# Reordered opening, accumulators in pairs of PSUM banks, and one wide VectorE rescale in a macaron feed-forward / S4 kernel

## The chip, the cores and the metric

The kernel runs on one core of one Trainium2 chip. The metric is the device time of one execution in microseconds (us), from the first to the last instruction and the little that lies around them. A change of 0.2% or less can't be told from none here.

## The reference

The input u has shape (2, 1024, 1024). Read as 2048 rows of 1024, it goes through three residual parts: half of a gated feed-forward of the layer-normed input, an S4 sequence convolution of the layer-normed input, and the same feed-forward again.

```python
def _dequant(qweight, scales, qzeros, g_idx):
    shifts = jnp.arange(PACK, dtype=jnp.uint32) * BITS        # PACK 8, BITS 4
    w = (qw[:, None, :] >> shifts[None, :, None] & MAXQ).reshape(-1, qweight.shape[1])
    z = ((qz[:, :, None] >> shifts[None, None, :] & MAXQ) + 1).reshape(qzeros.shape[0], -1)
    return (w.astype(scales.dtype) - z[g_idx].astype(scales.dtype)) * scales[g_idx]
...
h = jax.nn.silu(xf @ Wg) * (xf @ Wu)                          # 1024 -> 2752
out = h @ Wd                                                  # 2752 -> 1024
...
y = jnp.fft.irfft(jnp.fft.rfft(u, n=n) * jnp.fft.rfft(K, n=n), n=n)[..., :L]
return y + D[0] * u                                           # K from the S4 parameters
...
x = x + 0.5 * _L0_ffn_ref(_layernorm(x, axis=-1), ...)
x = x + _L0_attn_ref(_layernorm(x, axis=-1), ...)
x = x + 0.5 * _L0_ffn_ref(_layernorm(x, axis=-1), ...)
```

The feed-forward weights are 4-bit, with a scale and a zero point for each group of 128 input rows (8 groups for gate and up; 21 for down, whose last 64 rows share the last group). Everything is in float32.

## The kernel before

**Jobs.** The 2048 rows are four blocks of 512 (`TB`). Each block passes the feed-forward twice, so there are eight jobs (`JOBS`, line 1069). Jobs 0, 1, 4, 5 are the first feed-forward of blocks 0 to 3, jobs 2, 3, 6, 7 the second. `fast()` walks through the jobs; each is a `gate_up` stage and a `down` stage. What lies between two feed-forwards of a block (moments, normalizing, transposes, convolution, saving) is hung as hooks on the steps of the neighbouring jobs' stages: `at(up, s, f)` runs f at step s of gate/up, `at(dn, d, f)` at step d of down. The convolution of jobs 1, 2, 5 and 6 is such a hook, and the S4 tables are built in job 1.

**Weights.** In job 0 the packed words are fetched (`fetch`, line 365), split into nibbles (`split`), and made into integers minus zero points (`dequantize`, line 391), without the scale. The result goes to DRAM (`w_q`), and each job reads it back tile by tile (`load_w`, three steps ahead, six buffers in `wpool`). The zero points are first turned from packed words to a table in DRAM (`zero_points`, line 209) and read back spread over the rows (`fetch_zeros`). Down weights follow the same way in hooks of job 0.

**Precision and scales.** Each activation is split in two pieces, `xTh` (fp32r) and `xTl` (the rest), so that each product is two matmuls of 128x128 by 128x512. The scale of a group is applied by Horner's rule on the accumulator in PSUM: after group g the accumulator is multiplied by the ratio `rat` of scale g to scale g+1 (`scaled`, line 475), and the matmuls of the next group add on top. So every step has matmul, rescale, matmul, rescale on one accumulator; ScalarE rescales at line 477, VectorE at line 479.

**Gate/up.** 43 columns of 128 (21 gate, 21 up, one of two halves of 64) are done in eight waves: five of three gate/up couples, three of two, the last with the half unit besides. A wave has eight steps, one for each group; a step has four to six units, gate and up in turn (`order`, line 493). A unit is an accumulator of one PSUM bank, 128x512 float32; the pool `acc` has six, the pool `ps` the other two banks, which transposes and small products use. Even units are rescaled by ScalarE, odd ones by VectorE; in job 0 also the odd unit at position 1 goes to ScalarE, except at g = 3. After the last group `gated` (line 521) makes silu of the gate accumulator on ScalarE, the product with the up accumulator on VectorE, and the two pieces on GpSimd.

**Down.** Two halves of 512 output columns, each 22 row blocks with four accumulators `po` (line 559), rescaled in the same way by `ratd`.

**The order of work.** [...] The order on each engine is set by a scheduler when the program is built, from priorities, dependencies and its own estimates, and it also places the waits on semaphores. It keeps track of which tile each instruction reads and writes. SP issues nearly all DMAs; in the opening ScalarE's queue issues some of them too.

**The opening** (lines 1160 to 1187) loads the zero-point words on ScalarE's queue (three DMAs into one tile, which GpSimd clears first), the block's four row tiles and the first packed words on SP's; then come moments, subtraction of the mean on ScalarE (`less_mean`), eight dequantizations of the first weight tile, whose first row is also stored straight into `first_tile` by ScalarE's queue (line 399), the scaling by the deviation, and the transposes (`turn`).

Of the kernel before, what the change touches and what calls it, by code (L numbers as in the profile page):

```python
# [9 lines left out]
F32 = mybir.dt.float32  # L10
# [5 lines left out]
ALU = mybir.AluOpType  # L16
AX = mybir.AxisListType
PSUM = bass.MemoryType.PSUM
DRAM = bass.MemoryType.DRAM
# [30 lines left out]
def macaron_s4_kernel(  # L50
# [43 lines left out]
    ypool = ctx.enter_context(tc.tile_pool(name="y", bufs=4))  # L94
    apool = ctx.enter_context(tc.tile_pool(name="acc", bufs=6, space=PSUM))
    ppool = ctx.enter_context(tc.tile_pool(name="ps", bufs=2, space=PSUM))
# [4 lines left out]

    def acc(name):
        return apool.tile([P, 512], F32, tag="acc", name=name)

# [8 lines left out]
    row_t = const.tile([P, 1], F32, tag="row", name="row_t")  # L113
    shift_t = const.tile([P, 1], I32, tag="shift", name="shift_t")


# [51 lines left out]

    def turned(n, half, name, bank=bank):

        ps = bank(name)
        for k in range(4):
            nc.tensor.transpose(ps[:, bass.ts(k, P)], n[:, bass.ts(4 * half + k, P)], ident)  # L173
        return ps.rearrange("p (c t) -> p c t", c=4)
# [4 lines left out]
    def turn(b, t, n, half, bank=bank):  # L179
        k = ln[b, t][2]  # L180
        if b not in pieces:
            pieces[b] = [
                xtpool.tile([P, NC, TB], F32R, tag="xT", name=f"xT{w}_{b}_{k}") for w in ("h", "l")
            ]
        hi, lo = (a[:, 4 * half : 4 * half + 4, bass.ts(t, P)] for a in pieces[b])
        ps = turned(n, half, f"pt_{b}_{k}_{t}_{half}", bank)
        nc.scalar.copy(hi, ps)  # L187
        nc.vector.tensor_tensor(lo, ps, hi.bitcast(F32), ALU.subtract)  # L188
# [19 lines left out]

    def zero_points():

        n, nd = INTER // 8 // SEG, HID // 8 // SEGD
        z = t2("zq").bitcast(I32)[:, : n + nd]
        nc.gpsimd.memset(z, 0)
        for i, src in enumerate((gate_qz, up_qz)):
            own = slice(GK * SEG * i, GK * SEG * (i + 1))
            nc.scalar.dma_start(z[own, :n], src.rearrange("g (s n) -> (g s) n", s=SEG))
        nc.scalar.dma_start(z[: GD * SEGD, n:], down_qz.rearrange("g (s n) -> (g s) n", s=SEGD))
        zi = t4("zi").bitcast(I32)[:, : 8 * (n + nd)]
        for k in range(8):
            nc.vector.tensor_scalar(  # L220
                zi.rearrange("p (a k) -> p k a", k=8)[:, k, :],
                z,
                4 * k,
                15,
                ALU.logical_shift_right,
                ALU.bitwise_and,
            )
        tab = t2("ztab").bitcast(BF16)[:, : 8 * (n + nd)]
        nc.vector.tensor_scalar(tab, zi, 1.0, None, ALU.add)
        nc.scalar.dma_start(z_dram.rearrange("g (s n) -> (g s) n", s=SEG), tab[:, : 8 * n])  # L230
        nc.scalar.dma_start(
            zd_dram.rearrange("g (s n) -> (g s) n", s=SEGD), tab[: GD * SEGD, 8 * n :]
        )

# [156 lines left out]
    def dequantize(w, j):  # L391

        parts, z = packed[w]
        q = wpool.tile([P, width_of(w)], F32R, tag="w", name=f"q_{w}_{j}")
        src = parts[j % 2][:, j // 2, :]
        nc.vector.tensor_tensor(q, src, z, ALU.subtract)  # L396
        dst = w_q[w].rearrange("(r j) n -> j r n", j=8)[j]
        if w == 0:
            nc.scalar.dma_start(first_tile[j:P:8].bitcast(F32), q[: P // 8].bitcast(F32))
        nc.sync.dma_start(dst, q.bitcast(F32))  # L400
        if j == 7:
            packed.pop(w)
# [31 lines left out]
    def first_weights(up, dn, at):  # L434


        for w in range(1, len(WAVES)):
            s0 = 8 * w - 12
            at(up, max(0, s0 - 3), lambda w=w: (fetch(w), fetch_zeros(w)))
            at(up, max(0, s0 - 1), lambda w=w: split(w))  # L440
            for j in range(8):
                s = s0 + j if w > 1 else (1, 2, 2, 3, 3, 3, 4, 4)[j]
                at(up, s, lambda w=w, j=j: dequantize(w, j))
        s0 = len(STEPS) - 12
        when = lambda n: (up, s0 + n) if n < 12 else (dn, (5 * (n - 12)) // 6)
        for n in range(6 * 8):
            k, j = divmod(n, 8)
            a, rt = divmod(k, 3)
            if j == 0:
                at(*when(max(0, n - 3)), lambda a=a, rt=rt: fetch_down(a, rt))  # L450
                at(*when(max(0, n - 1)), lambda a=a, rt=rt: split_down(a, rt))
            at(*when(n), lambda a=a, rt=rt, j=j: dequantize_down(a, rt, j))

    AHEAD = 3

    def load_w(j, s):
# [24 lines left out]
    def gate_up(j, b, hooks):  # L481
        hi, lo = pieces[b]
        ps = {}
        ready = {s: load_w(j, s) for s in range(AHEAD)}
        for s, (wi, g) in enumerate(STEPS):
            if s + AHEAD < len(STEPS):
                ready[s + AHEAD] = load_w(j, s + AHEAD)
            for hook in hooks.get(s, ()):
# [7 lines left out]
            for pos, (unit, col) in enumerate(order):  # L496
                if g == 0:
                    ps[unit] = acc(f"pg_{j}_{unit}")
                p = ps[unit]
                for k, part in enumerate((lo, hi)):  # L500
# [7 lines left out]
                    )  # L508
                if g < GK - 1:
                    on_act = unit % 2 == 0 or (j == 0 and pos == 1 and g % 4 < 3)  # L510
                    if unit == 2 * WIDE:
                        on_act = g % 2 == 0
                    scaled(on_act, p, p, rat[:, unit, g : g + 1])
                elif unit == 2 * WIDE:
# [33 lines left out]
    def down(j, b, hooks):  # L548
# [3 lines left out]
        for d, (a, f) in enumerate(steps):  # L552
# [5 lines left out]
            if f == 0:  # L558
                ps = [acc(f"po_{j}_{a}_{c}") for c in range(4)]
            for c in range(4):  # L560
# [284 lines left out]
    def turn_whole(n, name):  # L845
        s = t4(name).rearrange("p (c t) -> p c t", c=NC)
        for half in range(2):
            ps = turned(n, half, f"{name}_{half}")
            dst = s[:, 4 * half : 4 * half + 4, :]
            if half:  # L850
                nc.vector.tensor_copy(dst, ps)
            else:
                nc.scalar.copy(dst, ps)
# [5 lines left out]
    def general():  # L859
# [146 lines left out]
        def feed_forward(b, k):  # L1006
# [6 lines left out]
            for f in range(NF):  # L1013
                m = width(f)
                got = []
                for i in range(2):
                    ps = acc(f"pf_{b}_{k}_{f}_{i}")
                    for a in range(2):
# [3 lines left out]
                        for j in range(4):  # L1022
# [3 lines left out]
                            )  # L1026
                    got.append(ps)
                g = gpool.tile([P, TB], F32, tag="g", name=f"gf_{b}_{k}_{f}")
# [4 lines left out]
            for t0 in range(0, NT, 2):  # L1033
                ps = {(t, nh): acc(f"pd_{b}_{k}_{t}_{nh}") for t in (t0, t0 + 1) for nh in range(2)}
                for f in range(NF):
# [35 lines left out]
    def fast():  # L1071
        for j, (b, k) in enumerate(JOBS):
# [47 lines left out]
            if j == 0:  # L1120
                for s, k0, k1 in ((2, 3, 11), (12, 11, 19), (20, 19, WIDE)):
                    at(up, s, lambda k0=k0, k1=k1: scales(k0, k1, scale_rows(k0, k1)))
                at(up, 28, scales_down)
                for t in range(NT):
                    at(up, t, lambda t=t: turn(0, t, first[t], 1))
                first_weights(up, dn, at)
            if j == 1:
                tables = s4_tables()
                for s in range(2, 42):
                    at(up, s, lambda: next(tables, None))  # L1130
            if j == 2:
                at(up, 30, in_order)
            if after:
# [12 lines left out]
                for t in range(NT):  # L1146
                    at(dn, o + 1 + 4 * t, lambda t=t: anorm(t))
                    at(dn, o + 2 + 4 * t, lambda t=t: turn(ab, t, an[t], 0))
                    at(dn, o + 4 + 4 * t, lambda t=t: turn(ab, t, an[t], 1))
            at(dn, 21, lambda: load_x(b, rows_of(u, b) if k == 1 else saved(b)))  # L1150
# [8 lines left out]

    zero_points()  # L1160
    x[0] = [t4(f"x_0_{t}") for t in range(NT)]
    for t, src in enumerate(rows_of(u, 0)):
        nc.sync.dma_start(x[0][t], src)
        if t == 1:
            fetch(0)
    fetch_zeros(0)
    srow = scale_rows(0, 3, nc.scalar)
    first = []

    def less_mean(t, m):  # L1170

        n = t4(f"xn_0_1_{t}")
        nc.scalar.activation(n, x[0][t], AF.Identity, bias=m, scale=-1.0)
        first.append(n)
        if t == 1:
            split(0)

    moments(0, 1, less_mean)
    deviations(0, 1, -1.0)
    for i in range(8):  # L1180
        dequantize(0, i)
    scales(0, 3, srow)
    for t in range(NT + 1):
        if t < NT:
            nc.scalar.activation(first[t], first[t], AF.Copy, scale=ln[0, t][1])  # L1185
        if t:
            turn(0, t - 1, first[t - 1], 0, acc)
    x.pop(0)
# [87 lines left out]
```

## Time and profile before

| what | us |
|---|---|
| median of 3 runs | 2219.82 |
| lowest and highest | 2217.35, 2220.73 |
| the profiled execution, its own time | 2220.67 |
| its span, first to last instruction | 2218.9 |
| first product of gate/up starts at | 35.44 |
| gate/up of jobs 0 to 7 | 190.3, 214.5, 196.4, 159.9, 159.8, 194.6, 194.7, 159.8 |
| down of jobs 0 to 7 (the last with the end of the program) | 102.6, 86.0, 86.4, 86.5, 85.9, 86.0, 85.9, 94.2 |

The stage lengths are the distances between the first products of line 501 (gate/up) and line 562 (down) on TensorE's timeline. The profile is of one execution. Its page gives the busy time of each engine; a group's row has the line, the engine, the operation, output and input by name and shape, the count, the busy time and the mean in ns of one, then the idle time ahead of it and what ended most of that. A wait "A <- B" says that A stood idle until B was done. Matmuls are pipelined, so their durations overlap, and the distance of their starts says more than their sum.

### The profile page before, as it was taken

What the parts mean: (1) busy time and instruction counts of PE and PEld (TensorE: products, weight loads), DVE (VectorE), ACT (ScalarE), POOL (GpSimd) and SP (SyncE); (2) the same over time, 40 slices, a digit from 0 to 9 for tenths busy, and PEclk for the clock granted to TensorE, in tenths of its full rate; (3) what the DMA queues carried; (4) which work ended last, traced back from release to release, by engine and by line L of the source; (5) the groups of instructions that cost most, each with busy time, mean ns of one, the idle gap of its engine ahead of it and who ended that gap; (6) DMA issues with size and microseconds to landing.
All of it is one profiled execution on the core that took longest, in us unless ns stands there. A gap on an engine that the chain in (4) does not pass through costs nothing.

```text
span 2218.9 us, 28013 instructions
## 1 busy us (share of the span) xinstructions
PE 2134.2 (96%) x9364; PEld 1683.4 (76%) x9364; DVE 1712.8 (77%) x2792; ACT 1452.8 (65%) x2229; POOL 328.8 (15%) x350
## 2 busy tenths in 40 slices
PE   4898889999999999999999999999999999999998
PEld 3676667867887778888788878877788777888876
DVE  7898869767786878877887777867788677777776
ACT  5776776545764677677767777646676467767775
POOL 0232002211011230122102320102201023012210
PEclk9999999999999999999999999999999999999999
DMA  7788784434443545644455444434444354554444
GB/s 238 271 261 274 233 250 131 141 96 150 135 149 107 174 135 173 225 146 136 142 185 187 126 138 138 150 104 159 138 136 146 108 180 134 156 189 144 135 136 130
DMA packets 163667, 359.91 MB, mean 162 GB/s; under 512 B 22395, under 2 KB 27588, under 8 KB 163518
## 3 DMA queue, kind: packets, MB, share of 16 engines
q1 hardware_dynamic: 162730, 357.47, 51.8%
q8 instruction: 78, 1.28, 0.2%
q10 hardware_dynamic: 788, 0.58, 0.1%
q14 instruction: 71, 0.58, 0.1%
HBM read 306.86 MB, written 50.73 MB: 161 GB/s over the span
## 4 chain that ended last, share of the span: by engine, by line
PE 51%; issue 35%; DMA 5%; DVE 5%; POOL 3%; ACT 1%; SPq 0%; ACTq 0%; DVEq 0%; POOLq 0%
PE pg L501 35%; PE po L562 9%; PE pc L835 5%; POOL hl L530 2%; POOL hh L528 1%; DMA w<-wq 1%; DMA wd<-wdq 1%; DMA wdq<-qd 1%; DVE pg L479 1%; DVE hf L526 1%; DVE q L396 1%; PE st L173 1%; DMA wq<-q 1%; PE pt L173 0%; PE pb L583 0%
## 5 line engine op out<-in xcount | busy, mean ns | idle before, releaser
L477 ACT ACTIVATE pg<-pg,rat 128x512 f32<-128x512 f32 x1256 | 820.1, 662 | 467.0 <-PE pg L501 462.4
L501 PE MATMUL pg<-xTl,w 128*128 128x512 f32 x2752 | 1084.3, 396 | 27.9 <-DVE pg L479 12.2
L501 PE MATMUL pg<-xTh,w 128*128 128x512 f32 x2752 | 1070.9, 391 | 0.0
L479 DVE TENSOR_TENSOR pg<-pg,rat 128x512 f32<-128x512 f32 x1152 | 785.8, 696 | 162.9 <-PE pg L501 154.1
L501 PEld LDWEIGHTS pg<-xTl,w 128*128 128x128 f32 x2752 | 517.8, 188 | 164.1 <-DVE pg L479 22.6
L501 PEld LDWEIGHTS pg<-xTh,w 128*128 128x128 f32 x2752 | 518.6, 188 | 103.3 <-issue 0.2
L562 PE MATMUL po<-hl,wd 128*128 128x512 f32 x1344 | 538.2, 403 | 18.4 <-DVE po L479 7.7
L477 ACT ACTIVATE po<-po,ratd 128x512 f32<-128x512 f32 x670 | 438.7, 662 | 170.1 <-PE po L562 169.8
L562 PE MATMUL po<-hh,wd 128*128 128x512 f32 x1344 | 521.3, 392 | 0.0
L479 DVE TENSOR_TENSOR po<-po,ratd 128x512 f32<-128x512 f32 x610 | 419.1, 697 | 93.5 <-PE po L562 89.2
L528 POOL CAST hh<-hf 128x512 fp32r<-128x512 f32 x168 | 109.4, 651 | 1755.1 <-DVE hf L526 1630.5
L562 PEld LDWEIGHTS po<-hl,wd 128*128 128x128 f32 x1344 | 252.1, 188 | 96.4 <-DVE po L479 18.4
L562 PEld LDWEIGHTS po<-hh,wd 128*128 128x128 f32 x1344 | 253.4, 189 | 46.0
L530 POOL TENSOR_TENSOR hl<-hf,hh 128x512 fp32r<-128x512 f32 x168 | 222.9, 1327 | 13.5
L526 DVE SCALAR_TENSOR_TENSOR hf<-pg,rat,g 128x512 f32<-128x512 f32 x168 | 125.1, 748 | 78.6 <-PE pg L501 32.6
L523 ACT ACTIVATE g<-pg,rat 128x512 f32<-128x512 f32 x168 | 115.6, 689 | 41.8 <-PE pg L501 39.2
L835 PE MATMUL pc<-toeplitz,st 128*128 128x512 f32 (+3 forms) x384 | 126.5, 486 | 0.0
L835 PEld LDWEIGHTS pc<-toeplitz,st 128*128 128x128 f32 x384 | 70.3, 190 | 57.4 <-issue 46.0
L843 DVE TENSOR_TENSOR x<-x,pc 128x512 f32<-128x512 f32 x32 | 22.0, 686 | 77.4 <-PE pc L835 77.2
L137 DVE BATCH_NORM_STATS2 stats<-x 128x6 f32<-128x512 f32 x96 | 64.6, 679 | 2.2 <-DMA x<-in_L_attn_u_dram 1.1
L188 DVE TENSOR_TENSOR xTl<-pt,xTh 128x512 fp32r<-128x512 f32 x64 | 43.5, 685 | 17.3 <-ACT xTh L187 17.3
L173 PE MATMUL pt<-ident,xn 128*128 128x128 f32 x256 | 42.9, 286 | 14.1 <-ACT xn L1185 14.1
(135 smaller groups left out, 617.5 us busy)
## 6 DMA issues: line engine op xcount, KB each, us to landing
w<-wq SPq DMA_DIRECT2D x319, 384.0 KB
wd<-wdq SPq DMA_DIRECT2D x336, 256.0 KB
w<-wq SPq DMA_DIRECT2D x128, 256.0 KB
w<-wq SPq DMA_DIRECT2D x64, 320.0 KB
x<-in_L_attn_u_dram SPq DMA_DIRECT2D x32, 512.0 KB
wq<-q SPq DMA_DIRECT2D x40, 384.0 KB
wdq<-qd SPq DMA_DIRECT2D x32, 256.0 KB
xs<-x SPq DMA_DIRECT2D x16, 512.0 KB
```

The lines of the kernel that those rows point to most:

```text
L137: nc.vector.bn_stats(stats[:, t, i, :], x[b][t][:, bass.ts(i, 512)])
L173: nc.tensor.transpose(ps[:, bass.ts(k, P)], n[:, bass.ts(4 * half + k, P)], ident)
L188: nc.vector.tensor_tensor(lo, ps, hi.bitcast(F32), ALU.subtract)
L477: nc.scalar.activation(dst, src, AF.Copy, scale=sc)
L479: nc.vector.tensor_tensor(dst, src, sc.to_broadcast([P, TB]), ALU.mult)
L501: nc.tensor.matmul(p, w[:, bass.ts(col, P)], part[:, g, :], start=(g == 0 and k == 0), stop=(g == GK - 1 and k == 1), skip_group_check=True,)
L523: nc.scalar.activation(g, pg, AF.Silu, scale=rat[:, 2 * f, GK - 1 :])
L526: nc.vector.scalar_tensor_tensor(hf, pu, last, g, ALU.mult, ALU.mult)
L528: nc.gpsimd.tensor_copy(hi, hf)
L530: nc.gpsimd.tensor_tensor(lo, hf, hi.bitcast(F32), ALU.subtract)
L562: nc.tensor.matmul(ps[c], w[:, bass.ts(c, P)], part, start=(f == 0 and k == 0), stop=(f == NF - 1), skip_group_check=True,)
L835: nc.tensor.matmul(ps[:, lo - 512 * nh :], lhsT(c), toeplitz[:, lo - P * c : end - P * c], start=(c == 0), stop=(c == last),)
```

## The change

- The pool `acc` has three buffers of 128x1024 in place of six of 128x512. `accs` hands out a tile of two banks as two halves. Gate and up of one couple are the two halves of one tile; in down, accumulators 0 and 1 are one tile, 2 and 3 another. The half unit of the last wave takes a bank of the pool `ps`.
- In waves of three couples of job 0, positions 4 and 5 get no rescale of their own: after position 5 one VectorE operation multiplies both halves, 2x512 columns, by their two ratios. Position 3 goes from VectorE to ScalarE.
- The opening works on half-width tiles (512 columns), splits the zero points in a part for gate/up and one for down, which comes at step 24, puts two of the four row tiles on ScalarE's queue and all first-tile stores on SP's, fetches the packed words of wave 1 before the loop, and moves the second halves of the transposes to hooks of the first steps. Later steps: the scales come in three pieces of six couples at other steps, two tiles of weights are loaded ahead in job 0 in place of three.
- `in_order_of_writing` ties the instructions that a function writes, on the engines named, to the order in which they are written: the opening and the second halves on ScalarE, VectorE and SP, the fetches on SP, the splits on VectorE, the S4 tables of job 1 on VectorE and ScalarE.

```diff
-    apool = ctx.enter_context(tc.tile_pool(name="acc", bufs=6, space=PSUM))
+    apool = ctx.enter_context(tc.tile_pool(name="acc", bufs=3, space=PSUM))
...
-    def acc(name):
-        return apool.tile([P, 512], F32, tag="acc", name=name)
+    def accs(name):
+
+        both = apool.tile([P, 1024], F32, tag="acc", name=name)
+        return [both[:, bass.ts(i, 512)] for i in range(2)], both
...
+    def in_order_of_writing(f, *engines):
+
+        start = len(nc.cur_bb.bb.instructions)
+        f()
+        written = list(nc.cur_bb.bb.instructions)
+        for e in engines:
+            last = next((i for i in reversed(written[:start]) if i.engine == e), None)
+            for ins in written[start:]:
+                if ins.engine == e:
+                    if last is not None:
+                        tc.add_manual_dep(
+                            ins,
+                            last.name,
...
+    def zero_words(which):
+
+        if which:
+            n = HID // 8 // SEGD
+            z = t2("zq_1").bitcast(I32)[: GD * SEGD, :n]
+            nc.sync.dma_start(z, down_qz.rearrange("g (s n) -> (g s) n", s=SEGD))
+            return z
...
         if w == 0:
-            nc.scalar.dma_start(first_tile[j:P:8].bitcast(F32), q[: P // 8].bitcast(F32))
+            nc.sync.dma_start(first_tile[j:P:8].bitcast(F32), q[: P // 8].bitcast(F32))
         nc.sync.dma_start(dst, q.bitcast(F32))
...
-                s = s0 + j if w > 1 else (1, 2, 2, 3, 3, 3, 4, 4)[j]
+                s = s0 + j if w > 1 else (1, 2, 2, 3, 3, 4, 4, 5)[j]
...
     def gate_up(j, b, hooks):
         hi, lo = pieces[b]
-        ps = {}
-        ready = {s: load_w(j, s) for s in range(AHEAD)}
+        ps, pairs = {}, {}
+        ahead = AHEAD if j else FIRST
+        ready = {s: load_w(j, s) for s in range(ahead)}
...
-                if g == 0:
-                    ps[unit] = acc(f"pg_{j}_{unit}")
+                if g == 0 and unit == 2 * WIDE:
+                    ps[unit] = bank(f"pg_{j}_{unit}")
+                elif g == 0 and unit % 2 == 0:
+                    (ps[unit], ps[unit + 1]), pairs[unit // 2] = accs(f"pg_{j}_{unit}")
...
-                if g < GK - 1:
-                    on_act = unit % 2 == 0 or (j == 0 and pos == 1 and g % 4 < 3)
+                if g < GK - 1 and j == 0 and n == 3 and pos >= 4:
+                    if pos == 5:
+                        both = pairs[unit // 2].rearrange("p (u t) -> p u t", u=2)
+                        sc = rat[:, unit - 1 : unit + 1, g : g + 1].to_broadcast([P, 2, TB])
+                        nc.vector.tensor_tensor(both, both, sc, ALU.mult)
+                elif g < GK - 1:
+                    on_act = unit % 2 == 0 or (j == 0 and pos == 1 and g != 3)
                     if unit == 2 * WIDE:
                         on_act = g % 2 == 0
+                    if j == 0 and n == 3 and pos == 3:
+                        on_act = True
                     scaled(on_act, p, p, rat[:, unit, g : g + 1])
...
-                ps = [acc(f"po_{j}_{a}_{c}") for c in range(4)]
+                ps = [p for c in (0, 2) for p in accs(f"po_{j}_{a}_{c}")[0]]
...
-                for s, k0, k1 in ((2, 3, 11), (12, 11, 19), (20, 19, WIDE)):
+                for s, k0, k1 in ((4, 3, 9), (20, 9, 15), (36, 15, WIDE)):
                     at(up, s, lambda k0=k0, k1=k1: scales(k0, k1, scale_rows(k0, k1)))
-                at(up, 28, scales_down)
+                at(up, 24, lambda: zero_points(1, zero_words(1)))
+                at(up, 40, scales_down)
                 for t in range(NT):
-                    at(up, t, lambda t=t: turn(0, t, first[t], 1))
+                    at(up, t, lambda t=t: in_order_of_writing(lambda: second_half(t), *STARTING))
...
                 for s in range(2, 42):
-                    at(up, s, lambda: next(tables, None))
+                    piece = lambda: next(tables, None)
+                    at(up, s, lambda: in_order_of_writing(piece, ET.DVE, ET.Activation))
...
+    def start():
+        zeros = zero_words(0)
+        x[0] = [t4(f"x_0_{t}") for t in range(NT)]
+        for t, src in enumerate(rows_of(u, 0)):
+            (nc.sync, nc.scalar)[t // 2].dma_start(x[0][t], src)
+        fetch(0)
+        srow = scale_rows(0, 3)
+        fetch(1)
+        zero_points(0, zeros)
+        fetch_zeros(0)
+        fetch_zeros(1)
...
+        moments(0, 1, then)
+        deviations(0, 1, -1.0)
+        for i in range(8):
+            dequantize(0, i)
+        banks = [p for i in range(2) for p in accs(f"turn_{i}")[0]]
+        for t in range(NT + 1):
+            if t < NT:
+                by_deviation(t, 0)
+            if t:
+                turn(0, t - 1, first[t - 1, 0], 0, lambda name: banks[t - 1])
+        for t in range(NT):
+            less_mean(t, 1)
+        scales(0, 3, srow)
+
+    in_order_of_writing(start, *STARTING)
```

## The prediction

> **What bounds the kernel now.** I read the page first, then the table of stages, then the waits, then the timeline of a place where TensorE starves. In the table the columns are length, then busy time (count) of TensorE, its weight loads, VectorE, ScalarE, GpSimd; the rows are the opening, the first job's gate/up and down stages, and a plain later job (number 3, counted from 0).
>
> ```profile
> PE 2134.2 (96%) x9364; PEld 1683.4 (76%) x9364; DVE 1712.8 (77%) x2792; ACT 1452.8 (65%) x2229; POOL 328.8 (15%) x350
> ```
>
> ```profile
> 0.00:35.40 35.40, 5.82 (x27) 5.07 (x27) 20.86 (x58) 12.92 (x15) 0.84 (x8) 1.00 0.72 235
> 35.40:225.70 190.30, 171.62 (x724) 129.30 (x724) 163.64 (x252) 140.95 (x224) 47.88 (x40) 0.99 0.80 267
> 225.70:328.30 102.60, 91.92 (x393) 68.03 (x393) 78.02 (x160) 75.48 (x123) 2.01 (x3) 0.98 0.76 238
> ...
> 911.60:1071.50 159.90, 159.38 (x705) 130.19 (x705) 123.05 (x182) 114.93 (x174) 35.42 (x38) 1.00 0.53 167
> 1071.50:1158.00 86.50, 85.57 (x394) 68.41 (x393) 72.33 (x123) 59.15 (x93) 3.71 (x4) 1.00 0.53 161
> ```
>
> From job 3 on TensorE is never idle: 159.4 of 159.9 us. Only the first 328 us have slack to win: 30 us in the opening, 19 in gate/up, 11 in down. The waits of job 3 (total, times, longest):
>
> ```profile
> ACT pg L477 <- PE pg L501: 40.2, 144, 1.1
> DVE pg L479 <- PE pg L501: 25.3, 113, 0.7
> ```
>
> Both rescalers wait for TensorE, not the other way. That works because six accumulators circulate independently: TensorE needs 0.455 us for one (two matmuls, starts at 1001.10, 1001.56, 1002.01 in the timeline), so it comes back after 6 x 0.455 = 2.73 us, while the trip through a rescale is shorter. How short is seen where TensorE had to wait, in the first wave:
>
> ```profile
> 59.22 1.28 DVE L479 TENSOR_TENSOR pg<-pg,rat 128x512 f32<-128x512 f32 x2
> ...
> 59.96 0.50 PE L501 MATMUL pg<-xTl,w 128*128 128x512 f32 x1 [0.57 <-DVE pg L479]
> ...
> 60.30 0.40 PE L501 MATMUL pg<-xTh,w 128*128 128x512 f32 x1
> ...
> 60.73 0.70 DVE L479 TENSOR_TENSOR pg<-pg,rat 128x512 f32<-128x512 f32 x1 [0.23 <-PE pg L501]
> ...
> 61.48 0.50 PE L501 MATMUL pg<-xTl,w 128*128 128x512 f32 x1 [0.20 <-DVE pg L479]
> ```
>
> Released at 59.96, the two matmuls end at 60.70 (0.74), VectorE runs 60.73 to 61.43, TensorE is released at 61.48. One trip with VectorE is 1.52 us; with ScalarE, by its row, 0.04 less:
>
> ```profile
> L477 ACT ACTIVATE pg<-pg,rat 128x512 f32<-128x512 f32 x1256 | 820.1, 662 | 467.0 <-PE pg L501 462.4
> L479 DVE TENSOR_TENSOR pg<-pg,rat 128x512 f32<-128x512 f32 x1152 | 785.8, 696 | 162.9 <-PE pg L501 154.1
> ```
>
> [...]
>
> **The pair of banks, in every stage.** The diff says only that two accumulators share one tile. The listing of the built program's waits says what follows. These are TensorE's matmuls into one pair in job 3, a wave of three pairs (names shortened):
>
> ```
> pg_3_12 <-xTl, w_3_17 [waits DMAHW4, DVE]
> pg_3_12 <-xTh, w_3_17
> pg_3_12 <-xTl, w_3_17 [waits Activation]
> pg_3_12 <-xTh, w_3_17
> pg_3_12 <-xTl, w_3_18 [waits DMAHW5, DVE]
> ```
>
> The first two lines write the gate half, the next two the up half. Followed by the semaphore values, the up half waits for ScalarE's rescale of the gate half of the same step, and the next gate half for VectorE's rescale of the up half; before, each waited only for its own accumulator. The rescales carry the mirrored waits (ScalarE's, which waited for TensorE alone, waits for VectorE too). So the halves alternate: a step of a pair costs 1.48 + 1.52 = 3.00 us, however many engines are free. [...]
>
> Down: a half holds two pairs (four accumulators), TensorE's work per step is 4 x 0.455 = 1.82 us, the pair's trip 3.00. The built order runs them in lockstep (gate halves of both, then second halves), so 3.00 stands. 20 rescaled steps and about 1.6 us for the last ones make 61.6 per half; the second half starts about 3 steps early in the spare pair: 2 x 61.6 - 9 = 114. Casts, normalizing and additions of the next block (0.6 to 0.8 us each, some 20 per stage) that fall into a trip delay it: between 0 and 14 us, I take 5. So 119 against 86.2: +33 per job.
>
> Gate/up, five waves of three pairs: TensorE's order in most rounds is first pair's gate; half of the second's gate; third's up; the rest of the second's gate; first's up; then the same with the third split. A split unit takes 0.34 + 0.455 + 0.39 = 1.19 instead of 0.74, so its pair's trip is 1.19 + 0.74 + 0.66 + 0.70 + four hand-overs of 0.045 = 3.47. Bounds: 3.00 (the unsplit trip) and 3.9 (a stray VectorE operation in every round); I take 3.47. 40 rounds: 139. The last three waves have two pairs each; the order lets the next wave's first pair start 4 steps early, which gives 20 rounds in place of 24: 8 at 3.00, 12 with a third pair at 3.47: 66. Together 204 against 159.9: +44. With down +33: **+77 for jobs 3, 4, 7**. Jobs 2, 5, 6 carry the convolution, 34.8 us of TensorE (194.7 - 159.9); 16 rounds with 0.74 free take in some 10: +67 each. Job 1 has it in late waves with more free time, and the S4 tables (now in written order on VectorE and ScalarE): I hide 15: +63.
>
> **The wide rescale, job 0 only.** [...] ScalarE trades position 4 for position 3, nothing. The third pair needs one wait less, but ScalarE now serves four rescales: I take 3.3 a round. 40 x 3.3 + 66 = 198, plus a fourth of today's 34 us of stalls (190.3 - 43 x 8 x 0.455), since the rest fits in the waiting: 207 against 190.3, +17 (bounds 0 and +45). Its down stage has 36 dequantizing operations on VectorE beside the trips, 0.3 us of delay for each: 130 against 102.6, +27.
>
> **The opening.** Half-width passes, two zero-point DMAs on ScalarE's queue in place of three, x on two queues, the second block's weights fetched before the zero points, and the eight first-tile stores moved from ScalarE's queue to SP's, whose queue now issues all sixteen. Today ScalarE stands 11.4 us behind its own stores (scaling only at 27.5) and the first weight row comes at 16.35. With deviations ahead, eight dequantizations follow each other, the last at about 23; its store lands 4.5 us later: first product at 28 instead of 35.4. The second step's tile, written through the same SP queue and read back, is then late by 2 to 3. I take -5, bounds -10 and +8. The later zero points for down (step 24) and the smaller scale pieces lie beside TensorE's waits: 0. If that cover were missing, a few us. The half unit of the last wave takes one of two other banks; the transposes that then wait sit inside the 5 us above.
>
> Sum: -5 + 17 + 27 + 63 + 3 x 67 + 3 x 77 = +534. The profiled execution took 2220.67 (span 2218.9 and 1.8 around it), 0.04% from the median 2219.82: **2755**.
>
> **Rivals.** (1) Floor: the split order costs nothing, every round is 3.00. 52 rounds x 0.47 x 7 jobs, 12 less in job 0, and its 0.3 x 40: 2755 - 189, about 2570. For it: queues may slip into a better phase. Against: the order is fixed. (2) Heavy: side work lands in the trips; rounds of 3.9 and 3.3: (52 x 0.43 + 46 x 0.3) x 8 = +290: 3045. For it: VectorE is busy 77% with little spare inside a pair's trip. (3) The other side, faster: the waits are listed but satisfied before TensorE comes[...]. It needs a pair's trip below 2.73 us (1.82 in down); measured trips say 3.00, so it decides only if a wait in a waiting state costs far less than at 59.96.
>
> **How the numbers follow.** Forecast 0.62 (alone 2680 to 2850), floor 0.14, heavy 0.19, faster 0.04, within 0.2% (what a measurement can tell from no change) 0.01. The range 2590 to 2930 leaves out the far part of floor and heavy and the faster case. Slower 0.95.
>
> **What would show it.** TensorE's busy share falls to about 80%; its waits for the rescales, 0.5 us in job 3's gate/up, become tens of us, shared between ScalarE and VectorE; down stages last 115 to 130 us, gate/up about 200; [...] job 0 suffers least. Wrong if down stages stay near 86 us (then the waits don't bind), or if gate/up rounds stand at 3.0 or near 4.

## The result: slower by 661 us, and the profile after

The changed kernel takes 2881.38 us (median of 4 runs, 2880.89 to 2883.72) against 2220.28 for the kernel before in the same session: 1.298 times as long, 95% interval 1.2956 to 1.3001. Its profiled execution took 2880.89, with a span of 2879.1.

First the table of stages of the kernel after, columns as in the prediction (stretch, length, then busy time and count of TensorE, its weight loads, VectorE, ScalarE, GpSimd; granted clock, DMA share, GB/s). The rows are the opening, the first job's gate/up and down, and job 3's gate/up and down. Neighbouring jobs overlap now: job 3's first gate/up products start some 10 us ahead of its row, between the last down products of job 2.

```profile
0.00:35.20 35.20, 5.70 (x24) 4.02 (x24) 20.91 (x54) 12.05 (x18) 0.74 (x7) 1.00 0.67 224
35.20:252.80 217.60, 192.87 (x724) 121.39 (x723) 164.07 (x238) 143.27 (x225) 42.36 (x38) 0.99 0.73 235
252.80:395.00 142.20, 120.16 (x416) 62.51 (x415) 75.88 (x118) 82.55 (x132) 4.22 (x4) 1.00 0.58 177
1134.60:1331.30 196.70, 180.25 (x657) 111.12 (x656) 114.45 (x170) 101.29 (x160) 35.40 (x38) 1.00 0.42 128
1331.30:1471.70 140.40, 126.47 (x443) 67.77 (x443) 81.79 (x134) 68.06 (x107) 3.78 (x4) 1.00 0.38 110
```

The opening kept its length (35.2 against 35.4). Everything behind it is longer, and in a plain job (one without convolution and tables) the rescaling engines do no more than before: in job 3's two stages together VectorE works 196.2 us and ScalarE 169.4, against 195.4 and 174.1. The time is waiting. Job 3's waits show between whom:

```profile
ACT pg L511 <- PE pg L538: 91.2, 92, 2.5
DVE pg L513 <- PE pg L538: 76.4, 88, 1.8
ACT po L511 <- PE po L606: 55.2, 49, 1.8
PEld pg L538 <- DVE pg L513: 49.2, 95, 0.8
DVE po L513 <- PE po L606: 44.0, 47, 2.3
```

TensorE's weight loads now wait 95 times for a VectorE rescale, and in gate/up ScalarE waits 91.2 us for TensorE and VectorE 76.4, where it was 40.2 and 25.3 before. When everyone waits for everyone, no engine bounds the stage: a cycle of dependences does. The timeline shows it, one round of three pairs in job 3 (weight loads and ScalarE's rescales are left out):

```profile
1179.64 0.74 PE L538 MATMUL pg<-xTl,w 128*128 128x512 f32 x2 [0.18 <-DVE pg L513]
...
1180.21 0.63 PE L538 MATMUL pg<-xTh,w 128*128 128x512 f32 x2
...
1180.68 0.39 PE L538 MATMUL pg<-xTl,w 128*128 128x512 f32 x1
...
1180.72 0.70 DVE L513 TENSOR_TENSOR pg<-pg,rat 128x512 f32<-128x512 f32 x1 [0.46 <-PE pg L538]
...
1181.47 0.74 PE L538 MATMUL pg<-xTl,w 128*128 128x512 f32 x2 [0.17 <-DVE pg L513]
...
1182.55 1.38 DVE L513 TENSOR_TENSOR pg<-pg,rat 128x512 f32<-128x512 f32 x2 [1.13 <-PE pg L538]
...
1183.30 0.74 PE L538 MATMUL pg<-xTl,w 128*128 128x512 f32 x2 [0.18 <-DVE pg L513]
```

TensorE is released at 1179.64, 1181.47 and 1183.30, every 1.83 us, each time by VectorE; a round of six units (the accumulators of the three pairs, once each) is 3.66. Between two releases it starts six matmuls, at 0.2275 each 1.37 us of work. The same spacing of 1.81 to 1.84 comes back in all waves of three pairs of the job. Where only two do, at the end of gate/up and in down, VectorE's releases are 3.07 to 3.09 apart, nearly all of them.

The job totals, from the last down product of the job before (in job 0 from the first product) to the job's own last down product, show how evenly the loss lies:

| job | before | after | more | forecast |
|---|---|---|---|---|
| 0 | 292.6 | 359.4 | +66.8 | +44 |
| 1 | 300.5 | 379.2 | +78.7 | +63 |
| 2, 5, 6 | 282.9, 280.6, 280.6 | 360.5, 360.7, 360.6 | +77.6, +80.1, +80.0 | +67 each |
| 3, 4, 7 | 246.3, 245.7, 241.8 | 337.1, 338.7, 335.5 | +90.8, +93.0, +93.7 | +77 each |

### The profile page after: what moved, and what is told of

It reads as the page before. It is cut to its first block, busy times and chain, and to the rows that moved or that the text cites. A ratio compares the mean times of both kernels' runs of the same rounds, so it can differ in the third digit from the quotient of the medians.

```text
span 2879.1 us, 31186 instructions
## 1 busy us (share of the span) xinstructions
PE 2603.1 (90%) x9364; PEld 1527.9 (53%) x9364; DVE 1723.6 (60%) x2766; ACT 1430.0 (50%) x2237; POOL 325.8 (11%) x349
## 4 chain that ended last, share of the span: by engine, by line
PE 46%; issue 29%; DVE 13%; ACT 7%; POOL 3%; DMA 1%; DVEq 0%; SPq 0%; ACTq 0%; POOLq 0%
PE pg L538 30%; PE po L606 13%; DVE pg L513 7%; ACT po L511 3%; DVE po L513 3%; ACT pg L511 3%; PE pc L879 2%; POOL hl L574 2%; DVE hf L570 1%; POOL hh L572 1%; PE pt L196 1%; PE pb L627 0%; ACT g L567 0%; DMA w<-wq 0%; DVEq L513 0%
## 5 line engine op out<-in xcount | busy, mean ns | idle before, releaser
L538 PE MATMUL pg<-xTl,w 128*128 128x512 f32 x2752 | 1153.6, 445 | 118.1 <-DVE pg L513 59.9
L511 ACT ACTIVATE pg<-pg,rat 128x512 f32<-128x512 f32 x1256 | 799.6, 660 | 783.4 <-PE pg L538 774.5
L513 DVE TENSOR_TENSOR pg<-pg,rat 128x512 f32<-128x512 f32 x1082 | 735.9, 697 | 503.2 <-PE pg L538 481.3
L538 PE MATMUL pg<-xTh,w 128*128 128x512 f32 x2752 | 1014.0, 396 | 0.0
L538 PEld LDWEIGHTS pg<-xTl,w 128*128 128x128 f32 x2752 | 496.5, 188 | 612.6 <-DVE pg L513 283.9
L606 PE MATMUL po<-hl,wd 128*128 128x512 f32 x1344 | 633.8, 475 | 114.7 <-ACT po L511 43.8
L606 PE MATMUL po<-hh,wd 128*128 128x512 f32 x1344 | 527.6, 395 | 0.0
L574 POOL TENSOR_TENSOR hl<-hf,hh 128x512 fp32r<-128x512 f32 x168 | 216.1, 1286 | 13.4
L879 PE MATMUL pc<-toeplitz,st 128*128 128x512 f32 (+3 forms) x384 | 136.4, 486 | 0.0
L879 PEld LDWEIGHTS pc<-toeplitz,st 128*128 128x128 f32 x384 | 70.6, 189 | 42.2 <-issue 30.2
L550 DVE TENSOR_TENSOR pg<-pg,rat 128x1024 f32<-128x1024 f32 x35 | 43.0, 1230 | 23.6 <-PE pg L538 23.4
```

Source lines behind the costliest of these rows:

```text
L511: nc.scalar.activation(dst, src, AF.Copy, scale=sc)
L513: nc.vector.tensor_tensor(dst, src, sc.to_broadcast([P, TB]), ALU.mult)
L538: nc.tensor.matmul(p, w[:, bass.ts(col, P)], part[:, g, :], start=(g == 0 and k == 0), stop=(g == GK - 1 and k == 1), skip_group_check=True,)
L550: nc.vector.tensor_tensor(both, both, sc, ALU.mult)
L574: nc.gpsimd.tensor_tensor(lo, hf, hi.bitcast(F32), ALU.subtract)
L606: nc.tensor.matmul(ps[c], w[:, bass.ts(c, P)], part, start=(f == 0 and k == 0), stop=(f == NF - 1), skip_group_check=True,)
```

## The experiments

The theory under test: the loss comes from the pair of banks being one tile, so that the build orders the two halves one behind the other. Rivals: the reordered opening and its written orders, or the wide rescale, cost the time.

**Single banks in the changed kernel.** Everything else stays; the wide rescale becomes two of 512 columns.

```diff
-    apool = ctx.enter_context(tc.tile_pool(name="acc", bufs=3, space=PSUM))
+    apool = ctx.enter_context(tc.tile_pool(name="acc", bufs=6, space=PSUM))
...
-        both = apool.tile([P, 1024], F32, tag="acc", name=name)
-        return [both[:, bass.ts(i, 512)] for i in range(2)], both
+        return [apool.tile([P, 512], F32, tag="acc", name=f"{name}_{i}") for i in range(2)], None
...
```

> The changed kernel with six accumulators of one bank each again, handed out as before; positions 4 and 5 of job 0's waves of three get one VectorE rescale of 512 columns each. Theory (the halves of a pair wait for each other's rescale): all of the loss goes, plain jobs return to 246 us (gate/up 160, down 86), first product at 29 to 31 us since the transposes of the opening no longer wait for each other, total 2195 to 2222. Rival (the written order on the queues and the moved DMAs cost the time): still above 2600, with plain jobs near 337. Rival (the wide VectorE operation costs it): also back to about 2220, so this run does not tell it from the theory.

Measured: 2230.05 us, 1.0036 times before (1.0026 to 1.0046). The loss is gone but for 0.4%. In its table of stages job 3 looks as before:

```profile
914.50:1075.20 160.70, 160.17 (x709) 130.79 (x709) 123.16 (x182) 115.22 (x174) 35.44 (x38) 1.00 0.54 167
1075.20:1160.90 85.70, 84.71 (x391) 67.82 (x390) 72.19 (x122) 58.81 (x92) 3.72 (x4) 1.00 0.54 160
```

TensorE is busy 160.2 of 160.7 us. The total is above the 2195 to 2222 that were expected, and the trace shows where it went: the earlier first product (30.08 against 35.44) is given back. Job 0 takes 299.1 instead of 292.6, job 1 303.3 instead of 300.5. (The profiled execution, 2224.88, was the fastest of the twelve.)

**Pairs alone, in the kernel before.** The other half of the comparison: no new opening, no written order, no wide rescale.

```diff
-    apool = ctx.enter_context(tc.tile_pool(name="acc", bufs=6, space=PSUM))
+    apool = ctx.enter_context(tc.tile_pool(name="acc", bufs=3, space=PSUM))
...
-    def acc(name):
-        return apool.tile([P, 512], F32, tag="acc", name=name)
+    def accs(name):
+
+        both = apool.tile([P, 1024], F32, tag="acc", name=name)
+        return [both[:, bass.ts(i, 512)] for i in range(2)], both
...
```

> The kernel before with pairs of banks alone: its own opening, order and narrow rescales, no wide one. Theory (pair waits): the whole loss, 2860 to 2900, plain jobs 335 to 340 us. Rivals (written order and moved DMAs, or the wide operation): 2215 to 2230, since neither is in it.

Measured: 2874.47 us, 1.2933 times before (1.2914 to 1.2952). Pairs alone carry practically the whole loss: 652 of 661 us. The rest is a balance. Job 0 takes 367.8 us here and 359.4 in the changed kernel, job 1 takes 362.7 and 379.2. The written order of the S4 tables is the only edit inside job 1, so I put these 16.5 us down to it, and the 2.8 by which job 1 of the first run is longer than before; no run changed that order alone.

**Pairs without the wide rescale.** In the changed kernel, two rescales of 512 columns where it has one of 1024.

```diff
-                    if pos == 5:
-                        both = pairs[unit // 2].rearrange("p (u t) -> p u t", u=2)
-                        sc = rat[:, unit - 1 : unit + 1, g : g + 1].to_broadcast([P, 2, TB])
-                        nc.vector.tensor_tensor(both, both, sc, ALU.mult)
+                    scaled(False, p, p, rat[:, unit, g : g + 1])
```

> The changed kernel with two VectorE rescales of 512 columns in place of the wide one in job 0. Theory (pair waits): the third couple gets one more wait, a trip of 2 x 1.52 in place of 2.7, so job 0 is the same or up to 15 us longer: 2880 to 2897. Rival (the wide operation costs the time): falls by hundreds of us, towards 2250.

Measured: 2880.31 us, 1.2962 times before (1.2944 to 1.2981), where the changed kernel stood at 1.2956 to 1.3001; job 0 takes 359.4 in both. The wide rescale is worth nothing that can be measured here. The group of the changed kernel says what it is:

```profile
L550 DVE TENSOR_TENSOR pg<-pg,rat 128x1024 f32<-128x1024 f32 x35 | 43.0, 1230 | 23.6 <-PE pg L538 23.4
```

1230 ns for one against 2 x 697 for two: 5.7 us of VectorE in all, and VectorE waited 23.6 us, nearly all of it for TensorE, ahead of these very operations. Work taken from an engine that waits there moved no end here.

**Matmuls written first.** Pairs stay, but the four matmuls of a couple are written ahead of its two rescales, in gate/up and in down. If the alternation is the cost, fewer alternations cost less.

```diff
+                late = [(unit, pos)]
+                if unit < 2 * WIDE:
+                    late = [(unit - 1, pos - 1), (unit, pos)] if unit % 2 else []
+                for unit, pos in late:
...
+                if c % 2 == 0:
+                    continue
+                for c in (c - 1, c):
```

> The changed kernel with the four matmuls of a couple written ahead of its two rescales, in gate/up and in down; pairs stay. Theory (pair waits): a step of a pair has one release of TensorE in place of two, 4 matmuls 1.19 us, ScalarE 0.66, VectorE 0.70 and hand-overs: 2.68 in place of 3.07 with two pairs, 2.75 to 2.95 in place of 3.66 with three (TensorE needs 2.73). About 60 us less per job: 2350 to 2480. Rival (order pins, moved DMAs, wide operation): unchanged, 2870 to 2890.

Measured: 2554.71 us, 1.1492 times before (1.1476 to 1.1509). The direction is right, but only 327 us come back, and the range was missed. The timeline of the down stage shows the trip:

```profile
1249.73 0.50 PE L611 MATMUL po<-hl,wd 128*128 128x512 f32 x1
...
1250.96 0.66 ACT L511 ACTIVATE po<-po,ratd 128x512 f32<-128x512 f32 x1 [0.65 <-PE po L611]
...
1251.66 0.70 DVE L513 TENSOR_TENSOR po<-po,ratd 128x512 f32<-128x512 f32 x1 [0.61 <-ACT po L511]
...
1252.36 0.66 ACT L511 ACTIVATE po<-po,ratd 128x512 f32<-128x512 f32 x1 [0.73 <-PE po L611]
1252.41 0.19 PEld L611 LDWEIGHTS po<-hl,wd 128*128 128x128 f32 x1 [0.53 <-DVE po L513]
```

VectorE, free for 0.61 us, waits for ScalarE, which works on the other bank of the same tile. So the two rescales of a couple don't run side by side, as the expectation's sum has it too. A couple's trip is therefore four matmuls, then 0.66, then 0.70: 2.68 us from 1249.73 to 1252.41, instead of 3.08. That is under the 2.73 that six accumulators give TensorE in a wave of three pairs: in job 3's gate/up TensorE runs through such a round without a wait, in 2.76 (1109.73 to 1112.49). It is over the 1.82 of two pairs, so down and the last waves still lose: job 3's down takes 114.6 us against 86.4 before, both from the last gate/up to the last down product. The trip, then, is as expected. What was too high is the 60 us that every job was to win: the plain jobs win 47 to 51, and jobs 0, 1, 2, 5 and 6, which carry other work besides, only 34 to 39.

**The small remainder.** Five runs on the single-bank version ask why the earlier opening doesn't show at the end. What stands ahead of TensorE in job 0's gate/up is a weight tile that has to be stored and read back; the totals of that wait in the first single-bank run and then in the last of these runs (before: 7.0 us):

```profile
PE pg L537 <- DMA w<-wq: 13.8, 7, 5.1
```

```profile
PE pg L537 <- DMA w<-wq: 11.3, 8, 3.2
```

First, three weight tiles ahead in job 0 as before, instead of two:

```diff
-                s = s0 + j if w > 1 else (1, 2, 2, 3, 3, 4, 4, 5)[j]
+                s = s0 + j if w > 1 else (1, 2, 2, 3, 3, 3, 4, 4)[j]
...
-    FIRST = 2
+    FIRST = 3
```

> Six single banks as in e1_single_banks, and in job 0 weights loaded three tiles ahead in place of two, with wave 1's dequantizations at the steps of the kernel before (the reader would else come too early). Theory (what the opening gains, 5.4 us, job 0 gives back in waits for weight tiles, 13.8 us in place of 7.0): job 0 gets 4 to 9 us shorter, total 2220 to 2226. Rival (the written order of the hooks gives it back): unchanged, 2228 to 2232.

Measured: 2237.47 us, 1.0061 (1.0045 to 1.0078). A miss: job 0 grows to 309.6. A longer lead is no remedy in this form; since the eight dequantizations moved with it, the run doesn't tell what the lead alone does.

Second, the written order kept for the opening alone (`start`), and dropped for the second half-width pass, the later fetches and splits, and the S4 tables:

```diff
-                    at(up, t, lambda t=t: in_order_of_writing(lambda: second_half(t), *STARTING))
+                    at(up, t, lambda t=t: second_half(t))
...
-                    at(up, s, lambda: in_order_of_writing(piece, ET.DVE, ET.Activation))
+                    at(up, s, lambda: piece())
```

> Six single banks as in e1_single_banks, and the written order kept for the opening alone: fetches, splits, second halves and S4 tables are free for the scheduler. Theory (two tiles ahead are the cause): job 1 loses its 2.8 us, job 0 stays within 2 us, total 2225 to 2229. Rival (the written order of the hooks is the cause): job 0 falls by 5 us or more besides, total 2217 to 2223.

Measured: 2226.24 us, 1.0019 (1.0009 to 1.0028). The total fits, the way there doesn't quite: the first product moves back to 35.95, while job 0 shrinks to 296.3, 2.8 less than in the first run and so between the two expectations, and job 1 to 301.5.

Third, a pair where the wide rescale needs one and single banks everywhere else:

```diff
+                    get = pair if j == 0 and n == 3 and pos == 4 else accs
+                    (ps[unit], ps[unit + 1]), pairs[unit // 2] = get(f"pg_{j}_{unit}")
```

> As e1_single_banks, but in job 0's gate/up one tile of two banks for the third couple of a wave of three, rescaled by one VectorE operation of 1024 columns as in the changed kernel, four single banks for the rest; six single banks from job 0's down stage on. Theory (the wide operation is harmless, the pairs elsewhere are the loss): total 2222 to 2234[...]. Rival (the wide operation pays where VectorE paces job 0): job 0 falls by 5 us or more, 2218 to 2225. Rival (the pair's release at a wave's end costs): above 2236.

Measured: 2231.59 us, 1.0045 (1.0032 to 1.0058); the intervals of this run and of the first overlap. No gain of the wide rescale can be measured in this place either.

Last, two runs together. In both the written order is kept for the opening, for the second half-width pass and for the first splitting, and dropped for the later fetches, splits and the S4 tables. The second also brings the scale rows in at steps 4, 12, 20 and 28, nearly as the kernel before did (its steps are 2, 12, 20 and 28; the expectation says 4 for the first):

```diff
-                for s, k0, k1 in ((4, 3, 9), (20, 9, 15), (36, 15, WIDE)):
+                for s, k0, k1 in ((4, 3, 11), (12, 11, 19), (20, 19, WIDE)):
...
-                at(up, 40, scales_down)
+                at(up, 28, scales_down)
```

> Single banks with the new opening; the hand-written order is kept for the opening and for what belongs to it in the first stage (the second half-width pass and the first splitting of weights), and dropped for the later weight fetches and splits and for the S4 tables in job 1. If the written order of the opening is what brings the first product to 30.1 us and the later written order is what costs job 0 and job 1 their few us, the first product stays at 30 to 31, job 0 takes 295 to 297 and job 1 300 to 302: 2219 to 2224 in all, no slower than before. If the first job's end is set by the stream of weights, job 0 takes up the earlier start and still ends near 328 us: 2224 to 2229, and nothing is won by opening earlier.

> As the run beside it, with the scale rows of the first stage brought in as in the kernel before (steps 4, 12 and 20, then 28 for the down scales, where the change has 4, 20, 36 and 40). If the later scale pieces (waits of 3.4 us for the ratio table show in the run with single banks) cost job 0 time, it gains 2 to 4 us on the run beside it; if job 0's end is set by the stream of weights, it is within 1 us of it.

Measured: 2225.52 us, 1.0009 (1.0003 to 1.0016), and 2221.34 us, 0.9995 (0.9986 to 1.0004). The first products come at 31.16 and 30.57, job 0 takes 302.9 and 299.5, job 1 301.7 and 300.3. The first of the two missed what was expected of job 0 either way: it took neither 295 to 297 us nor ended near 328, but at 334.1. So some 4 us (4.2 between the medians) hang on the time at which the scale rows come, though the two intervals touch. The best version with the new opening is level with the kernel before, not ahead: its job 0 still ends at 330.1, against 328.1, though it starts 4.9 us earlier. No version beat the kernel before.

The traces show where most of the earlier start goes. In the first single-bank run TensorE waits 5.06 us for a weight tile in job 0, and the clock granted to it is half (0.50, the third figure from the end) in this stretch:

```profile
200.30:207.10 6.80, 4.96 (x12) 3.93 (x13) 3.37 (x7) 1.70 (x3) 1.89 (x3) 0.50 0.92 305
```

```profile
202.14 0.77 PE L537 MATMUL pg<-xTl,w 128*128 128x512 f32 x1 [5.06 <-DMA w<-wq]
...
203.13 0.63 PE L537 MATMUL pg<-xTl,w 128*128 128x512 f32 x1
203.55 0.63 PE L537 MATMUL pg<-xTh,w 128*128 128x512 f32 x1
...
207.52 0.39 PE L537 MATMUL pg<-xTh,w 128*128 128x512 f32 x1
207.75 0.39 PE L537 MATMUL pg<-xTl,w 128*128 128x512 f32 x1
```

Matmuls start 0.43 us apart here, and 0.23 apart after it. Job 0 has 42 starts with the wide spacing in this run and 43 in the last one, against 14 in the kernel before. At 0.2 us each, 28 and 29 more of them are 5.6 and 5.8 us (an estimate), while TensorE's waits within job 0 grew only from 29.3 us to 31.3 and 30.2; job 0 is 6.4 and 6.9 us longer. In job 0 of the kernel before the profile has two such stretches: the granted clock is 0.51 from 211.1 to 214.5, after a wait of 2.04 us ahead of 209.92, and 0.52 from 231.5 to 234.9, after one of 1.91 us ahead of 231.02. Behind the wait of 2.14 us ahead of 82.01 it is 1.00 (82.0 to 85.4). Each trace is one execution, and no run was made to test this.

## Why the prediction was right, and where its sizes were off

**The pair of banks: right.** Halves that wait for each other were the named mechanism. Two runs settle it from both sides: pairs alone make 1.2933, single banks take the loss away. (The latter take out the wide rescale too; the run with pairs and two narrow ones shows that this isn't what helps.) It comes from the tile, not from the banks: the first single-bank run uses six banks side by side, with TensorE busy for 160.2 of 160.7 us in job 3's gate/up. There ScalarE rescales one accumulator from 1002.46 to 1003.12 and VectorE another from 1002.91 to 1003.61, while TensorE starts matmuls into a third at 1002.71 and 1002.94. The forecast's total was 127 us short of the measured +661. The measured time lies in the stated range, but above the 2680 to 2850 of the forecast alone; all errors went the same way, so none hid another. They are some 47 us in jobs 3, 4 and 7 together, 37 in jobs 2, 5 and 6, 16 in job 1, 23 in job 0 and 5 in the opening. These terms were mis-sized:

- **The round of three pairs, 3.47 in the prediction, is 3.66.** I followed one pair, whose split unit lengthens its trip. What binds goes across two pairs: released at 1179.64, TensorE runs one matmul of the split unit (0.34), then the two of the other pair's second half (from 1179.98), VectorE rescales that half (1180.72 to 1181.42), and this releases the other pair's split unit at 1181.47. Two such halves of 1.83 make the round. Over 52 rounds this is 9.9 us a job, most of the 14 to 17 missing in jobs 3, 4 and 7 and of the 11 to 13 in jobs 2, 5 and 6.
- **The step of down, 3.00, is 3.08**: 3 us over 40 steps. Job 3's down, counted from the last gate/up product, takes 126.2 (119 in the forecast), gate/up 210.9 (204); both boundaries are soft, since down's first products start 13.8 us before the last of gate/up.
- **Job 1's tables.** I hid 15 us of waiting for convolution and tables together and got +63. Pairs alone give +62.2 there. The other 16.5, by the comparison above, are the written order of the tables, for which I had added nothing.
- **Job 0**: gate/up +27 instead of +17, down +40 instead of +27. Waves 2 to 5 take 27.4 to 28.5 us for eight rounds, 3.4 to 3.6 a round where I took 3.3. The stalls that I let a fourth of stay, and the 36 dequantizing operations at 0.3 us each, may have cost more than I took as well; these parts were not measured apart.
- **The opening, -5, is -0.25.** Here the step that failed is the sentence that the waiting transposes "sit inside the 5 us". The opening's transposes use pairs as well, so a transposing group waits for VectorE to empty the other half of its tile, and VectorE is held by the dequantizations of the written order. In the timeline of the opening after:

```profile
24.34 0.96 DVE L425 TENSOR_TENSOR q<-raw,z 128x768 fp32r<-128x768 uint8 x1 [0.75 <-DMA wq<-q]
...
25.21 0.69 DVE L211 TENSOR_TENSOR xTl<-turn,xTh 128x512 fp32r<-128x512 f32 x1
...
25.95 1.11 PE L196 MATMUL turn<-ident,xn 128*128 128x128 f32 x4 [4.73 <-DVE xTl L211]
...
29.57 1.11 PE L196 MATMUL turn<-ident,xn 128*128 128x128 f32 x4 [2.50 <-DVE xTl L211]
```

TensorE stood 4.73 and 2.50 us for these, in the third and fourth of the four groups. With single banks the first product does come 5.4 us earlier, but job 0's end, which I let move with it, does not: the second half of that step fell too.

**The wide rescale: its effect on the round was wrong.** It takes 1230 ns. I let it, with one wait less, shorten job 0's rounds from 3.47 to 3.3, some 7 us in 40 rounds; the run without it has the same 359.4 us for job 0.

**The signs named ahead.** Tens of us of waits for rescales, down at 115 to 130 (job 3: 126.2) and job 0 suffering least (+66.8) came as written. TensorE's busy share did not:

```profile
PE 2603.1 (90%) x9364; PEld 1527.9 (53%) x9364; DVE 1723.6 (60%) x2766; ACT 1430.0 (50%) x2237; POOL 325.8 (11%) x349
```

I expected 80%; the page says 90%, for the same 9364 matmuls that took 2134.2 us before. A matmul is recorded with 0.39 us though the next starts after 0.23. In a stream the records overlap; ahead of a wait the last one counts in full. In the half round above 1.66 of 1.83 us count as busy (91%), where 1.37 are work (75%).

**The rivals.** The floor (rounds of 3.00) and the heavy case (3.9) are both refuted by the even 1.83. The faster case needed a pair's trip below 2.73 us. Of the runs with pairs only the one with matmuls written first has that, and there TensorE hardly waits in waves of three pairs: eight rounds take 23.2 to 23.4 us in job 3, against 22.0 in the kernel before.

**Open.** What makes job 0 give back the earlier start: the time of the scale rows is some 4 us of it, and stretches at half clock fill most of the difference in the traces. What brings the longer waits for weight tiles that remain (11.3 against 7.0), and the further stretches at half clock, has not been traced to one cause.

## What to carry to other kernels

What is rotated should be what is waited for: two accumulators that are used independently belong in two tiles, even where one wide operation would like them in one. Before merging buffers, list the waits of the built program, and compare the trip of one buffer (write, rescale, hand-overs) with the time the writer needs to come round; the smaller number of independent buffers has to cover it. And work out a round of waits across all buffers in the engine's actual order: the binding cycle can run through two of them.

## What the runs showed that was not expected

- A wait inserted between two engines on different banks of one tile also ties the two rescaling engines to each other: VectorE waited for ScalarE 0.61 us in the run with matmuls first, though neither needs the other's data.
- The clock stood many short waits, but not all of the longer ones. In job 3 of the changed kernel, with waits of 0.2 to 0.8 us by the tens in each stage, the granted clock stayed at 1.00. In the first single-bank run half clock comes with the wait of 5.06 us shown above (0.50), and with one of 1.94 us ahead of 234.38, in a down stage with a mean granted clock of 0.97.
- The written order of the S4 tables goes with 2.8 us more in job 1 with single banks, and with 16.5 under pairs. An order that engines with free buffers hardly notice may be paid in full once they wait for each other; this is read from a comparison, not tested alone.
